# Loading the convolution's weights later and in fewer bytes, and spreading them with smaller copies

## The chip, the cores and the metric

The kernel runs on one core of one Trainium2 chip. The metric is the device time of one execution in microseconds (us); for the kernel before it is 83.28 us, the median of three runs (83.2 to 83.3). The profiled execution took 83.26 us, of which the profile's span covers 82.0 us; times inside the trace are counted from the start of that span.

## The reference

Eight images of 32 channels and 128 x 128 pixels are normalized in 16 groups of two channels each, convolved with a 3 x 3 kernel by way of a 256 x 256 Fourier transform, given a bias and added to the input:

```python
def _gn(v, G=16, eps=1e-5):
    g = v.reshape(B_, G, C_ // G, H_, W_)
    m = jnp.mean(g, axis=(2, 3, 4), keepdims=True)
    s = jnp.var(g, axis=(2, 3, 4), keepdims=True)
    return ((g - m) / jnp.sqrt(s + eps)).reshape(v.shape)

def _L0_conv_ref(x, weight, bias, stride, padding):
    ...                                  # fft_H = fft_W = 256
    fout = jnp.einsum('bihw,oihw->bohw', fx, wf)
    sp = jnp.fft.ifft2(fout, norm='ortho').real
    sh = (fft_H - out_h) // 2            # 64: the crop begins at row and column 64
    out = sp[:, :, sh:sh + out_h, sw:sw + out_w]
    return out + bias[None, :, None, None]

x = x + _L0_conv_ref(_gn(x), L0_conv_weight, L0_conv_bias, 1, 1)
```

Because of the crop, the convolution reaches only a top left quarter (66 x 66) of each output image. Everywhere else the result is the input plus the bias.

## The kernel before

The host splits each image into its four phases (even and odd rows, even and odd columns). A partition is one phase of one channel, so an image is 128 partitions by 64 x 64 numbers. The 3 x 3 convolution becomes four 128 x 128 matrices (`w_sb`, 128 x 512), each used on 33 x 33 positions. Each matrix has the taps of the 3 x 3 kernel at fixed places, repeated for the four output phases, and zeros elsewhere.

On one side the SyncE queue loads the images, on the other the ScalarE queue loads `wb_sb` with the weights and the bias. Its columns are 5 x 3 taps of 32 outputs (the host repeats two rows of taps and puts in a row of zeros, so that each copy below is one regular pattern), the bias and 15 columns of zeros: 32 rows of 496 float32, 62 KB.

```python
loaded[0] = []
for half in range(2):
    rows = slice(half * H // 2, (half + 1) * H // 2)
    loaded[0].append((rows.stop, load(xts[0][:, rows, :], x[0, :, 0, rows, :])))
    if half == 0:
        weights_in = load(wb_sb, wb, by="act")        # the weights: first on ScalarE's queue
for img in range(1, 4):
    loaded[img] = [(H, load(xts[img], x[img // 2, :, img % 2]))]
for pair in range(2, NPAIR):
    loaded[2 * pair] = loaded[2 * pair + 1] = [(H, load(pairs[pair], x[pair]))]
# ... GpSimd builds avg, the matrix that averages over a group's partitions ...
put("act", lambda e: e.activation(warm, eps, AF.Sqrt), eps_ok)   # ScalarE's first activation
```

Then the first image is summed (VectorE: sums; ScalarE: sums of squares), `group` averages over the partitions with a matmul, `take_std` and `normalize` give `g`. In between GpSimd spreads the weights:

```python
pilot(0)                # a matmul on image 0's first pixel
pilot_back(0)           # ScalarE: its result, as an origin for the squares
sum_up(0)               # VectorE, two halves
sum_squares(0)          # ScalarE, two halves
keep_warm(0, 2)         # TensorE: filler matmuls 128 x 512 on avg
group(0, 0)
taps = wb_sb[:, 0 : 15 * C].rearrange("p (a b o) -> p a b o", a=5, b=3)
w5 = w_sb.rearrange("p (dr dc r k) -> p dr dc r k", dr=2, dc=2, r=2)
places = {0: ((0, slice(0, 1), slice(2, 3)), (1, slice(0, 2), slice(0, 2))),
          1: ((0, slice(0, 2), slice(1, 3)), (1, slice(1, 2), slice(0, 1)))}
w_zero = put("pool", lambda e: e.memset(w_sb, 0.0), mark=True)
for q in range(4):                                   # one band of 32 partitions per phase
    rin, cin = q // 2, q % 2
    to = slice(q * C, (q + 1) * C)
    bias_ok = put("pool", ... tensor_copy(bias_sb[to, :], wb_sb[:, 15 * C : 15 * C + 1]), weights_in)
    for dc, c, b in places[cin]:
        w_ok = put("pool", ... tensor_copy(w5[to, :, dc, :, c.start * C : c.stop * C],
                   taps[:, 1 - rin : 5 - rin, b, :]...), w_zero, weights_in)
group(0, 1)
warm_ok = keep_warm(0, 1, w_ok)  # one more filler matmul, only once the weights are spread
pilot(1)                         # needs image 1
take_std(0)                      # ScalarE square, VectorE var, ScalarE std, VectorE rstd, shift
normalize(0)                     # ScalarE, g in two pieces
# ... then, image after image: four products for each of three chunks, addition of ps and bias
# on VectorE, the rest of the image plus bias on GpSimd, the store on SyncE's queue ...
```

The steady part is a loop over the images: TensorE multiplies image i while ScalarE and VectorE sum image i + 2 and normalize image i + 1, and finished images are stored. The last image is stored in parts; the last store waits for the last addition on VectorE.

Of the kernel before, what the change touches and what calls it, by code (L numbers as in the profile page):

```python
# [153 lines left out]
def conv_preact_kernel(nc: bass.Bass, x: bass.AP, wb: bass.AP, out: bass.AP):  # L154
    NPAIR, _, _, H, W = x.shape
    B = 2 * NPAIR
    C = P // 4
# [7 lines left out]
    def sbuf(name, *shape):  # L165
        return nc.alloc_sbuf_tensor(name, list(shape), F32).ap()
# [4 lines left out]
    put = Queues(nc)  # L171
# [1 line left out]
    pairs = [sbuf(f"x{pair}", P, 2, H, W) for pair in range(NPAIR)]  # L173
    xts = [pairs[img // 2][:, img % 2] for img in range(B)]


    wb_sb = sbuf("wb_sb", *wb.shape)
    loaded = {}

    def load(to, of, by="sp"):  # L180
        name = f"load{len(put.sems)}"
        put.semaphore(name)
        return put(by, lambda e: e.dma_start(to, of), adds=name)  # L183

    loaded[0] = []
    for half in range(2):
        rows = slice(half * H // 2, (half + 1) * H // 2)
        loaded[0].append((rows.stop, load(xts[0][:, rows, :], x[0, :, 0, rows, :])))
        if half == 0:
            weights_in = load(wb_sb, wb, by="act")  # L190
    for img in range(1, 4):
        loaded[img] = [(H, load(xts[img], x[img // 2, :, img % 2]))]
    for pair in range(2, NPAIR):
# [12 lines left out]
    half = sbuf("half", P, 2 * C)  # L206
# [3 lines left out]
    bias_sb = sbuf("bias_sb", P, 1)  # L210
# [3 lines left out]
    for step, base in ((-1, 0), (1, 1)):  # L214
# [6 lines left out]
            pair_ok, mark=True,  # L221
# [12 lines left out]
        pair_ok, mark=True,  # L234
    )

    put("act", lambda e: e.activation(warm, eps, AF.Sqrt), eps_ok)  # L237

    gs = [sbuf(f"g{k}", P, N, N) for k in range(2)]

# [70 lines left out]
    def group(img, part=0):  # L311


        last = len(parts(img)) - 1
        of = to_sum(img, part)
        ok = put(
            "pe",
            lambda e: e.matmul(  # L318
                ps_ms[:, 0 : of.shape[1]], avg, of, start=(part == 0), stop=(part == last)
            ),  # L320
            *(sums_ok[img][part :: last + 1]), *([first_ok[img + 1]] if img and img + 1 < B else []),
            avg_ok, *means_read.get(img - 1, ()), mark=part == last,
        )
        if part == last:
            group_ok[img] = ok
# [117 lines left out]
    def keep_warm(first, times, *needs):  # L443
# [14 lines left out]

    taps = wb_sb[:, 0 : 15 * C].rearrange("p (a b o) -> p a b o", a=5, b=3)
    w5 = w_sb.rearrange("p (dr dc r k) -> p dr dc r k", dr=2, dc=2, r=2)
    places = {

        0: ((0, slice(0, 1), slice(2, 3)), (1, slice(0, 2), slice(0, 2))),
        1: ((0, slice(0, 2), slice(1, 3)), (1, slice(1, 2), slice(0, 1))),
    }
    w_zero = put("pool", lambda e: e.memset(w_sb, 0.0), mark=True)
    for q in range(4):
        rin, cin = q // 2, q % 2  # L470
        to = slice(q * C, (q + 1) * C)
        bias_ok = put("pool", lambda e: e.tensor_copy(bias_sb[to, :], wb_sb[:, 15 * C : 15 * C + 1]), weights_in, mark=True)
        for dc, c, b in places[cin]:
            w_ok = put(
                "pool",
                lambda e: e.tensor_copy(  # L476
                    w5[to, :, dc, :, c.start * C : c.stop * C],
                    taps[:, 1 - rin : 5 - rin, b, :].rearrange("p (dr r) b o -> p dr r (b o)", dr=2),
                ),
                w_zero, weights_in, mark=True,  # L480
            )
    group(0, 1)
    warm_ok = keep_warm(0, 1, w_ok)
    pilot(1)
# [41 lines left out]
    xt, to = xts[B - 1], out[NPAIR - 1, :, 1]  # L526
# [67 lines left out]
```

## Time and profile before

| engine | busy us | share of the span |
|---|---|---|
| TensorE, matmuls | 66.8 | 81% |
| VectorE | 50.2 | 61% |
| ScalarE | 47.9 | 58% |
| GpSimd | 31.6 | 39% |
| the 16 DMA engines, SyncE's queue alone | | 96.3% |

Busy time is the time in which an engine worked on an instruction, from its first to its last; a share is over the whole span. The DMA line is the time that the packets of a queue took, as a share of 16 engines times the span. The page also has a picture of the span in 40 slices (about 2.05 us each), where each digit is a busy share in tenths, and the trace can be asked for the same numbers over any stretch of time.

In the lines below, PE is TensorE's matmuls and PEld its weight loads, DVE is VectorE, ACT is ScalarE, POOL is GpSimd, SP is SyncE; a q behind the name is the engine's sequencer, which issues DMAs. L476 is line 476 of the kernel. `w_sb<-wb_sb 32x128` is an instruction that writes `w_sb` from `wb_sb` over 32 partitions and 128 elements in each. In square brackets stands how long the engine was idle before, and what ended it. A wait for several semaphores is put down to the one that came last in the record, which can be the wrong one.

### The profile page before, as it was taken

The page shows a single profiled execution, that of the slowest core. Times are in us where ns is not written, and L with a number is a line of the kernel's source. Part 1 is how long each engine was busy: PE and PEld are TensorE (multiplying, and loading weights), DVE is VectorE, ACT ScalarE, POOL GpSimd, SP SyncE. Part 2 cuts the span into 40 slices and gives each one's busy share as a digit, 9 for nine tenths or more (in the row PEclk, how much of TensorE's full clock was granted, in tenths as well). Part 3 has the DMA queues.
Part 4 walks back from the last instruction along what each step waited for, and adds up shares of the span by engine and source line. Part 5 has one row for each costly group of instructions (what it writes and reads, how often), then busy time and mean ns, then how long its engine had stood idle before and what let it go on. Part 6 is the DMA issues. An engine that isn't in the chain of part 4 may idle for free.

```text
span 82.0 us, 686 instructions
## 1 busy us (share of the span) xinstructions
PE 66.8 (81%) x222; PEld 41.3 (50%) x222; DVE 50.2 (61%) x43; ACT 47.9 (58%) x53; POOL 31.6 (39%) x43
## 2 busy tenths in 40 slices
PE   0009974999999999999999999999999999993000
PEld 0005433566666666666666656666666666660000
DVE  0009936960899499769949995996899324006000
ACT  3307967981699299569947974994798260000000
POOL 6876000004069900106992930490085029400000
PEclk9999998579999999999999999999999999999965
DMA  2899999999979979979959889989979999999995
GB/s 40 299 415 443 463 415 423 447 407 423 551 304 511 479 320 479 511 336 431 511 256 511 383 383 511 447 352 479 463 336 423 423 431 439 431 423 419 397 430 239
DMA packets 2164, 33.62 MB, mean 410 GB/s; under 512 B 296, under 2 KB 330, under 8 KB 500
## 3 DMA queue, kind: packets, MB, share of 16 engines
q1 hardware_dynamic: 2020, 33.36, 96.3%
q0 software_dynamic: 96, 0.19, 0.6%
q10 hardware_dynamic: 48, 0.06, 0.3%
HBM read 16.84 MB, written 16.78 MB: 410 GB/s over the span
## 4 chain that ended last, share of the span: by engine, by line
PE 74%; DMA 14%; DVE 2%; SPq 1%; issue 0%
PE ps L412 73%; DMA x<-x_dram 14%; DVE x L428 2%; PE ps_m L318 1%; SPq L183 1%; PE ps_w L265 0%
## 5 line engine op out<-in xcount | busy, mean ns | idle before, releaser
L412 PE MATMUL ps<-g,w_sb 128*128 128x363 f32 (+1 forms) x192 | 60.7, 473 | 0.1
L412 PEld LDWEIGHTS ps<-g,w_sb 128*128 128x128 f32 x192 | 36.1, 194 | 20.0 <-ACT origin L292 1.4
L283 DVE TENSOR_REDUCE sums<-x 128x1 f32<-128x4096 f32 x7 | 30.9, 4411 | 0.6 <-DMA x<-x_dram 0.6
L394 POOL TENSOR_SCALAR x<-x,bias_sb 128x1984 f32<-128x1984 f32 (+3 forms) x12 | 23.2, 1945 | 18.9 <-ACT origin L292 14.6
L303 ACT ACTIVATE unused<-x,origin 128x4096 f32<-128x4096 f32 (+1 forms) x9 | 30.0, 3330 | 0.3
L428 DVE SCALAR_TENSOR_TENSOR x<-ps,bias_sb,x 128x1089 f32<-128x1089 f32 (+2 forms) x9 | 10.9, 1220 | 7.7 <-PE ps L412 7.7
L373 ACT ACTIVATE g<-x,rstd 128x1089 f32<-128x1089 f32 (+2 forms) x8 | 9.4, 1190 | 3.4 <-DVE rstd L347 3.4
L283 DVE TENSOR_REDUCE first_sums<-x 128x1 f32<-128x2048 f32 x2 | 4.6, 2286 | 6.2 <-DMA x<-x_dram 6.2
L258 POOL COPY sums<-x 128x1 f32<-128x1 f32 x6 | 1.0, 186 | 18.2 <-DMA x<-x_dram 18.2
L335 DVE TENSOR_SCALAR var<-ps_m,square 128x1 f32<-128x1 f32 x8 | 1.8, 219 | 8.2 <-ACT square L330 8.2
L265 PE MATMUL ps_w<-x,avg 128*128 128x1 f32 x4 | 0.9, 304 | 7.1 <-POOL w_sb L476 6.1
L330 ACT ACTIVATE square<-ps_m,origin 128x1 f32<-128x1 f32 x8 | 2.1, 261 | 7.3 <-PE ps_m L318 7.3
L447 PE MATMUL ps<-x,avg 128*128 128x512 f32 x6 | 4.9, 942 | 0.0
L265 PEld LDWEIGHTS ps_w<-x,avg 128*128 128x128 f32 x4 | 0.8, 248 | 7.9 <-POOL w_sb L476 6.1
L318 PEld LDWEIGHTS ps_m<-sums,avg 128*128 128x128 f32 x16 | 2.8, 188 | 2.2 <-DVE x L428 1.0
L341 ACT ACTIVATE std<-var,eps 128x1 f32<-128x1 f32 x8 | 2.4, 294 | 2.3 <-DVE var L335 2.3
L344 DVE RECIPROCAL rstd<-std 128x1 f32<-128x1 f32 x8 | 1.3, 164 | 2.9 <-ACT std L341 2.9
L292 ACT ACTIVATE origin<-ps_w 128x1 f32<-128x1 f32 x2 | 0.3, 160 | 4.0 <-PE ps_w L265 4.0
L476 POOL COPY w_sb<-wb_sb 32x128 f32<-32x128 f32 (+1 forms) x8 | 2.5, 340 | 0.0
L318 PE MATMUL ps_m<-sums,avg 128*128 128x3 f32 x16 | 2.3, 214 | 0.0
L447 PEld LDWEIGHTS ps<-x,avg 128*128 128x128 f32 x6 | 1.5, 287 | 1.0 <-issue 1.0
L237 ACT ACT_TABLE_LOAD x1 | 1.3, 1283 | 1.2 <-PEq L579 1.2
(21 smaller groups left out, 13.3 us busy)
## 6 DMA issues: line engine op xcount, KB each, us to landing
x<-x_dram SPq DMA_DIRECT2D x2, 4096.0 KB, 34.3
out_dram<-x SPq DMA_DIRECT2D x2, 4096.0 KB
x<-x_dram SPq DMA_DIRECT2D x3, 2048.0 KB, 16.0
out_dram<-x SPq DMA_DIRECT2D x3, 2048.0 KB
x<-x_dram SPq DMA_DIRECT2D x2, 1024.0 KB, 6.2
out_dram<-x SPq DMA_DIRECT2D x1, 1056.0 KB
out_dram<-x SPq DMA_DIRECT2D x1, 800.0 KB
out_dram<-x POOLq DMA_DIRECT2D x1, 189.0 KB, 7.7
```

The lines of the kernel that those rows point to most:

```text
L283: lambda e: e.tensor_reduce(to_sum(img, k)[:, 0:1], piece, mybir.AxisListType.X, ALU.add),
L303: lambda e: e.activation(unused[:, rows.start * W : rows.stop * W], piece, AF.Square, bias=origins[img], accum_out=to_sum(img, k)[:, 1:2],),
L318: lambda e: e.matmul(ps_ms[:, 0 : of.shape[1]], avg, of, start=(part == 0), stop=(part == last)),
L330: lambda e: e.activation(squares[img], ps_ms[:, 0:1], AF.Square, bias=origins[img]),
L335: lambda e: e.tensor_scalar(variances[img], ps_ms[:, 1:2], squares[img], None, op0=ALU.subtract),
L341: lambda e: e.activation(stds[img], variances[img], AF.Sqrt, bias=eps, scale=float(FFT * FFT)),
L373: lambda e: e.activation(g[:, rows, :], xt[:, LO + rows.start : LO + rows.stop, LO:W], AF.Identity, bias=rstd[:, 1:2], scale=rstd[:, 0:1],),
L394: put("pool", lambda e: e.tensor_scalar(part, part, 1.0, bias_sb, op0=ALU.mult, op1=ALU.add), *free, mark=mark)
L412: lambda e, k=k, dc=dc, rows=rows, top=top: e.matmul(ps[:, 0:rows, 0 : N - dc], w_sb[:, k * P : (k + 1) * P], g[:, top : top + rows, dc:N] ...
L428: lambda e: e.scalar_tensor_tensor(part, in0=ps, scalar=bias_sb, in1=part, op0=ALU.add, op1=ALU.add),
L447: "pe", lambda e: e.matmul(pss[1][:, 0, :], avg, piece, start=True, stop=True),
L476: lambda e: e.tensor_copy(w5[to, :, dc, :, c.start * C : c.stop * C], taps[:, 1 - rin : 5 - rin, b, :].rearrange("p (dr r) b o -> p dr r ( ...
```

## The change

Three things are changed in the set-up of the weights, and nothing in the loop over the images. The load of `wb_sb` moves behind ScalarE's first activation. What is loaded shrinks to the nine taps and the bias, 32 rows of 289 float32, 37 KB. And since the repeated rows and the zeros are gone, each copy into `w_sb` is split in two by the place of the row: sixteen smaller copies on GpSimd take the place of eight. The four copies of the bias go from GpSimd to VectorE. It is meant to leave the transfer engines to the first image at the start, to move fewer bytes, and to take the bias off GpSimd's list.

```diff
     for half in range(2):
         rows = slice(half * H // 2, (half + 1) * H // 2)
         loaded[0].append((rows.stop, load(xts[0][:, rows, :], x[0, :, 0, rows, :])))
-        if half == 0:
-            weights_in = load(wb_sb, wb, by="act")
...
     put("act", lambda e: e.activation(warm, eps, AF.Sqrt), eps_ok)
 
+    weights_in = load(wb_sb, wb, by="act")
+
...
-    taps = wb_sb[:, 0 : 15 * C].rearrange("p (a b o) -> p a b o", a=5, b=3)
+    taps = wb_sb[:, 0 : 9 * C].rearrange("p (a b o) -> p a b o", a=3, b=3)
...
-        bias_ok = put("pool", lambda e: e.tensor_copy(bias_sb[to, :], wb_sb[:, 15 * C : 15 * C + 1]), weights_in, mark=True)
+        bias_ok = put("dve", lambda e: e.tensor_copy(bias_sb[to, :], wb_sb[:, 9 * C : 9 * C + 1]), weights_in, mark=True)
         for dc, c, b in places[cin]:
-            w_ok = put(
-                "pool",
-                lambda e: e.tensor_copy(
-                    w5[to, :, dc, :, c.start * C : c.stop * C],
-                    taps[:, 1 - rin : 5 - rin, b, :].rearrange("p (dr r) b o -> p dr r (b o)", dr=2),
-                ),
-                w_zero, weights_in, mark=True,
-            )
+            for dr, r, a in places[rin]:
+                w_ok = put(
+                    "pool",
+                    lambda e: e.tensor_copy(
+                        w5[to, dr, dc, r, c.start * C : c.stop * C],
+                        taps[:, a, b, :].rearrange("p a b o -> p a (b o)"),
+                    ),
+                    w_zero, weights_in, mark=True,
+                )
...
         "wb_dram": np.concatenate(
-            [
-                np.insert(weight.transpose(1, 2, 3, 0)[:, [1, 2, 0, 1]], 2, 0, axis=1).reshape(C, 15 * C),
-                np.asarray(L0_conv_bias).reshape(C, 1),
-                np.zeros((C, 15), x.dtype),
-            ],
-            axis=1,
+            [weight.transpose(1, 2, 3, 0).reshape(C, 9 * C), np.asarray(L0_conv_bias).reshape(C, 1)], axis=1
         ),
```

## The prediction

> **What bounds the kernel now.** I read the page's DMA part first, then the same transfers over stretches of time, then the first 14 us engine by engine. The queues, as packets, MB and share of 16 engines' span:
>
> ```profile
> span 82.0 us, 686 instructions
> ...
> q1 hardware_dynamic: 2020, 33.36, 96.3%
> q0 software_dynamic: 96, 0.19, 0.6%
> q10 hardware_dynamic: 48, 0.06, 0.3%
> HBM read 16.84 MB, written 16.78 MB: 410 GB/s over the span
> ```
>
> Queue 1 alone (images in and out) fills 96.3% of the span, all three 97.2%. That leaves 2.8%, or 2.3 us. Where they lie is seen by stretch: the columns are the stretch and its length, the busy time of PE, PEld, DVE, ACT and POOL, TensorE's clock, the DMA share and GB/s.
>
> ```profile
> 0.00:2.00 2.00, 0.00 (x0) 0.00 (x0) 0.00 (x0) 0.75 (x1) 1.25 (x8) 1.00 0.21 33
> 2.00:10.00 8.00, 3.90 (x6) 1.94 (x7) 3.81 (x2) 4.01 (x6) 4.85 (x16) 1.00 0.98 397
> 10.00:20.00 10.00, 8.39 (x26) 5.04 (x24) 5.78 (x5) 6.97 (x9) 0.92 (x2) 0.83 1.02 433
> ...
> 60.00:70.00 10.00, 10.00 (x36) 6.26 (x35) 5.73 (x7) 5.22 (x5) 5.67 (x4) 1.00 0.99 424
> 70.00:76.00 6.00, 4.54 (x17) 2.68 (x15) 1.42 (x2) 0.00 (x0) 0.72 (x2) 1.00 0.99 424
> ```
>
> From 2 us on the share is about 1.0 in every stretch, so the idle 2.3 us lie before the first packets and behind the last. The chain of waits names TensorE (74%) instead, because it follows the instructions back from the last store's issue; but that store, issued at 76.09 us, joins a queue that is still full. The tail shows it:
>
> ```profile
> 76.00:77.00 1.00, 0.00 (x0) 0.00 (x0) 0.06 (x1) 0.00 (x0) 0.00 (x0) 1.00 0.83 342
> 77.00:78.00 1.00, 0.00 (x0) 0.00 (x0) 0.00 (x0) 0.00 (x0) 0.00 (x0) 1.00 1.06 444
> 78.00:79.00 1.00, 0.00 (x0) 0.00 (x0) 0.00 (x0) 0.00 (x0) 0.00 (x0) 0.84 1.04 434
> 79.00:80.00 1.00, 0.00 (x0) 0.00 (x0) 0.00 (x0) 0.00 (x0) 0.00 (x0) 0.50 1.00 422
> ```
>
> After 76.09 us the engines move 0.91 x 342 + 444 + 434 + 422 kB, and another 482 kB after 80 us (the windows of that part give 456, 372 and 135 GB/s over half a us each): 2093 kB. The last store is 1056 KB, 1081 kB. So 1012 kB of older stores lay in front of it, 2.4 us at 420 GB/s. A new transfer needs some of this to get going: the first image load, issued at 0.81 us, moves nothing until 1.5 us and is moving by 2.0 us, so 0.7 to 1.2 us. The compute chain thus has 2.4 - 1.2, about 1 us, of slack at the end. The transfer engines set the time: start-up, then 33.6 MB, then the last landing.
>
> [...] 62 KB on ScalarE's queue landed 3.6 us after issue, while SyncE's half images took 6.2. [...] The granted clock was 0.50 from 14 to 16 us here[...]. [...] the reduction beside the weight copies and the one after them both took 2.29 us.
>
> **The change part by part.**
>
> First, bytes. The load falls from 62 KB to 32 x 289 x 4 = 36,992 bytes from 63,488. At 420 GB/s that is 26.5 kB / 420 = 0.06 us. By the page, queue 10 takes 0.3% of 82 us, 0.25 us (0.20 to 0.29 by its rounding); cut in proportion to the bytes (0.58) it saves 0.10 us. I take -0.08 us on a transfer time that is all on the path.
>
> Second, place. The issue leaves 0.81 us. ScalarE's table load and first activation, which ended at 2.74 us behind the 0.41 us issue, can end about 2.3 us; the issue follows then, or as early as 1 us if the sequencer does not hold it for the running activation. With the measured 3.6 us to landing: 4.6 to 5.9 us, 5.9 taken. In the changed kernel the first half image no longer has the weights in front of it and lands up to 63.5 kB / 420 = 0.15 us earlier; image 1 still has 37 KB in front and gains 0.06. The order of bytes is changed, their sum only by the 0.08 above.
>
> Third, the copies on GpSimd and who waits for them:
>
> ```profile
> 4.46 0.18 POOL L472 COPY bias_sb<-wb_sb 32x1 f32<-32x1 f32 x1 [0.46 <-DMA wb_sb<-wb_dram]
> 4.59 0.62 POOL L476 COPY w_sb<-wb_sb 32x128 f32<-32x128 f32 x2
> 5.27 0.18 POOL L472 COPY bias_sb<-wb_sb 32x1 f32<-32x1 f32 x1
> ...
> 7.00 0.63 POOL L476 COPY w_sb<-wb_sb 32x256 f32<-32x256 f32 x2
> ```
>
> The columns are start, length, instruction. From 4.46 to 7.63 us, 3.17 us in all; 0.81 us from band to band. By shape the means are 180 ns (1 element), 286 (128) and 394 (256): 0.844 ns an element on 180. The new copies are 32, 64, 64 and 128 elements a band: 206 + 233 + 233 + 287 = 959 ns. The old band sums to 860 ns and took 805, so three instructions overlap by 18 ns each; four give 959 - 72 = 887 ns. Four bands: 3.55 us, 0.38 more than before, although the bias copies are gone. With a landing at 5.9 us the last copy ends at 9.5 us instead of 7.63. Who waits is TensorE:
>
> ```profile
> 11.03 0.38 PE L318 MATMUL ps_m<-first_sums,avg 128*128 128x2 f32 x2 [0.53 <-ACT unused L303]
> 11.28 1.10 PE L447 MATMUL ps<-x,avg 128*128 128x512 f32 x2
> 13.39 0.38 PE L265 MATMUL ps_w<-x,avg 128*128 128x1 f32 x2 [1.00 <-DMA x<-x_dram]
> 13.84 0.94 PE L412 MATMUL ps<-g,w_sb 128*128 128x363 f32 x1
> ```
>
> The filler at 11.28 us is the first to need the weights, and it starts there because of the statistics in front of it. The convolution starts at 13.84 us because image 1 lands at 13.36. So 9.5 us is 1.8 us early. Even a filler moved to 12.29 us would end by 13.39.
>
> Fourth, the bias on VectorE. The copies stand behind both reductions, which end at 10.76 us, and in front of `var` at 11.75. The trace has a VectorE copy of one element at 145 ns; four make 0.58 us, to 11.34. `var` waits for ScalarE's square, which ends at 11.71, so 0.37 us remain; 0.3 if the chain comes earlier with image 0.
>
> Sum: bytes -0.08 us; place, GpSimd and VectorE 0.00, all beside other work. 83.28 - 0.08 = 83.2 us.
>
> **The rivals.** (A) The weights come late and a wait for them takes the place of the wait for image 1. For it: whole images with larger rows are queued by then, and the little transfer that GpSimd issues at 19.03 us lands only after 6.6 us. With 6.6 in place of 3.6 us the landing is 2.3 + 6.6 = 8.9, the copies end at 12.45, the filler at 13.55, so the convolution starts 0.16 us late[...]. Against it: that transfer is on the queue that the page calls software_dynamic, not on a hardware one. And about 1 us of slack at the end takes it up: 83.2 still. It would need a landing after 10 us to show, and then VectorE's in-order wait for the bias would hold `var` too; say 84.
>
> (B) The start-up gets shorter. From 1.5 to 3.0 us the windows show only 131, 139 and 158 GB/s, 214 kB where 420 GB/s would be 630, so 1.0 us is lost there, and the weight load is in it. If its small rows hold up the first image packets, moving it gives 0.1 to 0.4 us: 82.8 to 83.1. Against it: first packets have their own latency, and the 37 KB then land in full traffic, where nothing hides them. If the old ones were hidden in the ramp, the change costs up to 37 / 420 = 0.09 us instead: 83.4.
>
> (C) TensorE is the bound after all, as its 74% of the chain suggests. Then the time follows image 1's landing, 0.06 us earlier: 83.2 as well. A clock that changes around 14 us could move the compute chain by 1 us in either direction; only a delay above the slack would be seen.
>
> **Range and chances.** The centre is 83.2 us. (B) gives both ends, with repeated runs spread over 0.1 us: 82.9 to 83.5 us, 8 times in 10. The limits of 2% are 81.6 and 84.9 us. Nothing I find gives 1.6 us: faster 1%. Slower needs (A) with a landing after 10 us[...]: 2%. Within 2%: 97%.
>
> **What would show it.** In the changed profile: queue 10 at 0.04 MB and 0.1 to 0.2%; the DMA share still about 1.0 from 2 us to 80 us; GpSimd's sixteen copies over 3.4 to 3.7 us, ending by 10 us; the filler at about 11.2 us with the statistics, not the weights, in front of it; the bias copies between 10.6 and 11.4 us; `var` following the square at once; the convolution starting within 0.2 us of 13.8. It is wrong if the filler starts behind the last copy and the convolution with it, if `var` stands behind a bias copy, if the windows from 1.5 to 3 us move well over 214 kB, or if the DMA share has a hole before 80 us.

## The result and the profile after

The changed kernel takes 83.84 us (median of six runs, 83.8 to 84.24), the kernel before 83.22 (six runs of the same comparison): a ratio of 1.0081, 95% interval 1.0062 to 1.0100. It is 0.6 us slower, small but well outside the noise, and outside the predicted range of 82.9 to 83.5.

The page of the changed kernel, its span and its queues (packets, MB, share of 16 engines' span):

```profile
span 82.1 us, 695 instructions
...
q1 hardware_dynamic: 2020, 33.36, 96.3%
q0 software_dynamic: 96, 0.19, 0.6%
q10 hardware_dynamic: 48, 0.04, 0.1%
HBM read 16.81 MB, written 16.78 MB: 409 GB/s over the span
```

The first line is the riddle: the span is 82.1 us against 82.0, so the profiled program hardly changed while the measured time went up by 0.6. The queues are as foreseen. So are the stretches (length, busy PE, PEld, DVE, ACT, POOL, clock, DMA share, GB/s), full to the end:

```profile
10.00:20.00 10.00, 9.46 (x28) 5.72 (x27) 6.28 (x10) 7.14 (x11) 0.92 (x2) 1.00 1.02 436
...
60.00:70.00 10.00, 10.00 (x36) 6.25 (x35) 4.94 (x7) 4.43 (x5) 5.60 (x5) 1.00 0.99 423
70.00:76.00 6.00, 3.75 (x15) 2.16 (x13) 1.48 (x2) 0.00 (x0) 0.00 (x0) 1.00 0.99 423
```

And so is the set-up, in the timeline of the changed kernel (start, length, instruction, idle time in front):

```profile
0.95 0.38 ACTq L182 DMA_DIRECT2D wb_sb<-wb_dram  x1
...
5.19 3.33 POOL L476 COPY w_sb<-wb_sb 32x32 f32<-32x32 f32 x16 [1.19 <-DMA wb_sb<-wb_dram]
5.78 2.29 DVE L282 TENSOR_REDUCE first_sums<-x 128x1 f32<-128x2048 f32 x1 [5.78 <-DMA x<-x_dram]
...
10.47 0.66 DVE L471 COPY bias_sb<-wb_sb 32x1 f32<-32x1 f32 x4
...
11.26 2.06 PE L446 MATMUL ps<-x,avg 128*128 128x512 f32 x2
11.44 0.26 ACT L329 ACTIVATE square<-ps_m,origin 128x1 f32<-128x1 f32 x1 [0.68 <-PE ps_m L317]
11.74 0.22 DVE L334 TENSOR_SCALAR var<-ps_m,square 128x1 f32<-128x1 f32 x1 [0.60 <-ACT square L329]
...
13.63 5.54 PE L411 MATMUL ps<-g,w_sb 128*128 128x363 f32 x14
```

The copies end at 8.52 us, long before the filler at 11.26. The bias copies end at 11.13; `var` follows the square. The convolution starts at 13.63 us, 0.2 earlier than before. GpSimd waits longer for the weights (1.19 us against 0.46), but nothing on the way to the end does.

So the loss has to lie outside the span. The profiled executions took 83.26 us (before) and 83.80 (after); less 82.0 and 82.1 that leaves 1.3 and 1.7 us beside the span. The trace can be asked for stretches behind its last instruction. The changed kernel:

```profile
83.00:83.50 0.50, 0.00 (x0) 0.00 (x0) 0.00 (x0) 0.00 (x0) 0.00 (x0) 0.50 0.00 0
83.50:84.00 0.50, 0.00 (x0) 0.00 (x0) 0.00 (x0) 0.00 (x0) 0.00 (x0) 0.50 0.05 16
```

16 GB/s over half a us is 8 KB, about 1.7 us behind the last instruction of a kernel that has nothing left to move. The list of queues for 82 to 86 us says what it is:

```profile
DMA packets 1, 0.01 MB, mean 2 GB/s; under 512 B 0, under 2 KB 0, under 8 KB 0
## 3 DMA queue, kind: packets, MB, share of 16 engines
q14 instruction: 1, 0.01, 0.6%
```

A queue 14 of kind "instruction", one packet. (Both kernels have six such packets of 8 KB before the span starts.) The same question to the kernel before:

```profile
DMA packets 0, 0.00 MB, mean 0 GB/s; under 512 B 0, under 2 KB 0, under 8 KB 0
```

Theory T, a guess from that packet: an engine's instructions come in blocks of the packet's size; the change made one engine's stream longer, past the end of a block, and behind the span something then waits for the next block to be fetched. The trace records 686 instructions before and 695 after, waits and DMA issues included: four more on VectorE (45 to 49, the bias copies) and five more on GpSimd (58 to 63: eight copies more, four bias copies fewer, one wait more). Rivals: P, the later load itself costs; V, the bias copies on VectorE cost; N, each further instruction costs something outside the span. Of T the two traces show the packet and the counts. The block, the engine and the wait they do not show, nor a reason to expect 0.6 us.

### The profile page after: what moved, and what is told of

The parts are those of the page before. It is cut to its first block, busy times and chain, and to the rows that moved or that the text cites. A ratio compares the mean times of both kernels' runs of the same rounds, so it can differ in the third digit from the quotient of the medians.

```text
span 82.1 us, 695 instructions
## 1 busy us (share of the span) xinstructions
PE 67.3 (82%) x222; PEld 41.5 (51%) x222; DVE 50.7 (62%) x47; ACT 47.9 (58%) x53; POOL 31.8 (39%) x47
## 4 chain that ended last, share of the span: by engine, by line
PE 77%; DMA 9%; DVE 5%; SPq 0%; issue 0%
PE ps L411 72%; DMA x<-x_dram 9%; DVE first_sums L282 3%; PE ps L446 2%; PE ps_m L317 2%; DVE x L427 2%; PE ps_w L264 1%; SPq L182 0%; DVE bias_sb L471 0%
## 5 line engine op out<-in xcount | busy, mean ns | idle before, releaser
L446 PE MATMUL ps<-x,avg 128*128 128x512 f32 x6 | 5.8, 1108 | 0.0
L476 POOL COPY w_sb<-wb_sb 32x64 f32<-32x64 f32 (+2 forms) x16 | 3.2, 236 | 1.4 <-DMA wb_sb<-wb_dram 1.2
L317 PEld LDWEIGHTS ps_m<-first_sums,avg 128*128 128x128 f32 x4 | 1.2, 324 | 1.7 <-ACT unused L302 1.1
```

Source lines behind the costliest of these rows:

```text
L317: lambda e: e.matmul(ps_ms[:, 0 : of.shape[1]], avg, of, start=(part == 0), stop=(part == last)),
L446: "pe", lambda e: e.matmul(pss[1][:, 0, :], avg, piece, start=True, stop=True),
L476: lambda e: e.tensor_copy(w5[to, dr, dc, r, c.start * C : c.stop * C], taps[:, a, b, :].rearrange("p a b o -> p a (b o)"),),
```

## The experiments

All ratios are to the kernel before on the same chip, with 95% intervals, as recorded; they differ from the quotient of the two medians by up to 0.003. Each run's short diff is against the kernel before or, where said, the changed one.

**One part of the change alone, and length alone.** The load moved, the rest as before (e1_place):

```diff
-        if half == 0:
-            weights_in = load(wb_sb, wb, by="act")
...
     put("act", lambda e: e.activation(warm, eps, AF.Sqrt), eps_ok)
+    weights_in = load(wb_sb, wb, by="act")
```

> The kernel before with one part of the change: the 62 KB load moved behind ScalarE's first activation. Theory T (the lost 0.6 us lie behind the span, where an instruction fetch on queue 14 appeared because GpSimd's program grew from 58 to 63 instructions): the count is unchanged, so no fetch behind the span and 83.2 us. Rival P (the later load is the cause): 83.8 us.

Measured 83.26 us, ratio 0.9993 (0.9982 to 1.0004); no packet between 82 and 86 us. Rival P falls.

The bias copies on VectorE, the rest as before (e2_bias):

```diff
-        bias_ok = put("pool", ...
+        bias_ok = put("dve", ...
```

> The kernel before with one part of the change: the four copies of the bias on VectorE, so that VectorE's program grows by 4 instructions and GpSimd's shrinks by 4. Theory T with GpSimd as the engine: 83.2 us, no fetch behind the span. Theory T with VectorE as the engine, or rival V (bias copies on VectorE delay something): 83.8 us, and under T a fetch behind the span.

Measured 83.36 us, ratio 1.0003 (0.9991 to 1.0015); no packet. Rival V falls, and with it VectorE as T's engine.

The kernel before with five idle instructions more (e3_pool5):

```diff
         adds="moved",
     )
+    spare = sbuf("spare", P, 5)
+    for k in range(5):
+        put("pool", lambda e: e.memset(spare[:, k : k + 1], 0.0))
     sum_squares(1)
```

> The kernel before with nothing of the change, but five one-element memsets of a spare tile on GpSimd while it waits for image 2 (at about 19 us). Theory T with GpSimd as the engine: 83.8 us, the span within 0.1 us of 82.0, and one fetch of 8 KB on queue 14 about 1.7 us behind the span. Rivals P and V: 83.2 us, no fetch.

Measured 83.97 us, ratio 1.0079 (1.0061 to 1.0098): the whole loss, without any of the change. The five memsets take 0.25 us at 19.7 us, in a pause of GpSimd that lasts until 23.1. The span is 82.0 us, and behind it the queue list of this run shows

```profile
DMA packets 2, 0.02 MB, mean 4 GB/s; under 512 B 0, under 2 KB 0, under 8 KB 0
## 3 DMA queue, kind: packets, MB, share of 16 engines
q14 instruction: 2, 0.02, 1.5%
```

Two packets here against one in the changed kernel.

The changed kernel with its last five weight copies left out, which brings GpSimd back to 58 instructions and leaves parts of the matrices zero (e4_eleven; diff against the changed kernel):

```diff
             for dr, r, a in places[rin]:
+                copies += 1
+                if copies > 11:
+                    continue
                 w_ok = put(
```

> The changed kernel with eleven of its sixteen weight copies (the last five are left out, so a part of the matrices stays zero and the convolution is incomplete). GpSimd's program is back at 58 instructions; load, bytes and bias copies are those of the change. Theory T with GpSimd as the engine: 83.2 us and no fetch behind the span. Rivals P and V: 83.8 us.

Measured 83.25 us, ratio 0.9998 (0.9986 to 1.0011); no packet behind the span. The load's place, its 37 KB and the bias copies are all in it, and the loss is gone.

**Step or slope, and which engines.** The whole change, complete, with half of the weight copies moved to VectorE, 55 instructions on GpSimd (e5_split; diff against the changed kernel):

```diff
-                    "pool",
+                    "pool" if q < 2 else "dve",
...
-    warm_ok = keep_warm(0, 1, w_ok)
+    warm_ok = keep_warm(0, 1, half_ok, w_ok)      # half_ok: the last copy on GpSimd
...
```

> The whole change, complete, but with eight of the sixteen weight copies (the two bands of odd rows) on VectorE behind its two reductions, so that GpSimd's program has 55 instructions. Theory T with GpSimd's instruction stream as the cause: 83.2 us and no fetch behind the span; the copies hold up var by 0.5 to 1 us, which the slack at the end takes up. If the 0.6 us belonged to the change's work in any other way, 83.8 us. This run also says what the change is worth without the fetch: by the record -0.08 us, so a ratio of 0.999.

Measured 83.48 us beside 83.39 for the kernel before, ratio 1.0001 (0.9971 to 1.0030); no packet. The copies do delay the chain, by less than expected, as the timeline of this run shows:

```profile
11.54 0.50 DVE L476 COPY w_sb<-wb_sb 32x128 f32<-32x128 f32 x4
12.07 0.22 DVE L334 TENSOR_SCALAR var<-ps_m,square 128x1 f32<-128x1 f32 x1
```

`var` comes 0.32 us later than before (12.07 against 11.75), and nothing of it reaches the end. The interval is too wide to tell -0.08 us from nothing.

Three spare memsets instead of five (e6_pool3, the diff of e3_pool5 with 3):

> The kernel before with three spare memsets on GpSimd instead of five (61 instructions). If the cost is a step at a block of the instruction stream, the time is either 83.2 or 83.85 us and nothing between, the latter with a fetch on queue 14 behind the span. If every instruction costs something outside the span, 3/5 of 0.65: 83.6 us.

Measured 83.98 us, ratio 1.0064 (1.0047 to 1.0081), one packet on queue 14 behind the span. As much as with five: a step.

Six spare activations on ScalarE, and eighteen spare memsets on VectorE, each bringing its engine to 63 instructions (e7_act6, e8_dve18):

```diff
     put("act", lambda e: e.activation(warm, eps, AF.Sqrt), eps_ok)
+    spare = sbuf("spare", P, 6)                   # 18
+    for k in range(6):                            # 18
+        put("act", lambda e: e.activation(spare[:, k : k + 1], eps, AF.Sqrt))
+                                                  # "dve", e.memset(spare[:, k : k + 1], 0.0)
```

> The kernel before with six spare one-element activations on ScalarE behind its first one, where it is idle (57 + 6 = 63 instructions in its program, as many as GpSimd's in the changed kernel). If all engines have the same limit: 83.85 us and a fetch behind the span. If only GpSimd's stream stands close to a limit here: 83.2 us and no fetch.

> The kernel before with eighteen spare one-element memsets on VectorE before image 0 lands (45 + 18 = 63 instructions in its program). As with ScalarE: 83.85 us and a fetch behind the span if all engines have the same limit, 83.2 us if only GpSimd's stream stands close to one.

ScalarE: 83.39 us, ratio 0.9999 (0.9980 to 1.0019). VectorE: 83.65 us, ratio 1.0029 (1.0013 to 1.0045). Neither has an instruction packet behind the span, but each has one inside it, between 71 and 72 us and between 54 and 55 us. I had expected either the full step or nothing; the run on VectorE is between, and its loss is inside a span of 82.4 us. The limit of 58 is thus GpSimd's own in this kernel. Whether ScalarE or VectorE has such a step at another count stays open: VectorE went through 49 (e2_bias) and 57 (e5_split) without loss, and ScalarE was run with 57 and 63 only. Whose packets those two are, the traces don't say.

**How far beyond the limit.** One spare memset on GpSimd (e9_pool1), twenty (e10_pool20) and sixty (e11_pool60), by the diff of e3_pool5:

> The kernel before with one spare memset on GpSimd (59 instructions in its program). Theory T says only that the step lies between 58 and 61: either 83.2 us without a fetch behind the span or 83.85 us with one. A value between the two would speak for a cost per instruction.

> The kernel before with twenty spare memsets on GpSimd (78 instructions). If the cost comes from where the end of an 8 KB block falls, and the instructions that close the program behind the kernel's own are fewer than about 18, the end of the block now falls inside the span, the fetch moves there and is hidden: 83.2 to 83.5 us, a fetch on queue 14 before 82 us. If they are more, the time is 83.85 us with the fetch still behind the span. Rival N (any longer program costs more): at least 83.85 us, rather more than with five.

> The same with sixty spare memsets (118 instructions), which end near 23 us, before GpSimd's large additions are due. Block theory: the end of the block falls well inside the span, no fetch behind the span, 83.2 to 83.5 us, so more instructions cost less than five do. Rival N: more than 83.85 us.

One: 83.89 us, ratio 1.0060 (1.0039 to 1.0080). A single instruction in a pause (0.12 us, the mean of the sixty memsets in e11_pool60) cost 0.5 us. Its one profile was odd, with no packet of queue 14 behind the span and a span of 82.5 us. Twenty: 83.35 us, ratio 1.0000 (0.9979 to 1.0022). Twenty more instructions cost nothing where one cost half a us. The queue list of that run for 56 to 57 us shows where the packet went:

```profile
q1 hardware_dynamic: 15, 0.49, 114.6%
q14 instruction: 1, 0.01, 1.9%
```

It lies in the middle of the images' traffic, and none lies behind the span. Rival N falls. Sixty: 83.97 us, ratio 1.0048 (1.0024 to 1.0072), runs scattered from 83.37 to 84.36. The packet moved further forward, to between 23 and 24 us, as T with its blocks would have it, and the 1.2 us beside the span (84.2 less 83.0) are those of the kernel before. But the span of the profiled run was 83.0 us, and the twenty executions have spans from 82.1 to 83.1, so this kernel loses time inside, for a reason these runs don't show. My 83.2 to 83.5 us missed it.

**The same limit in the changed kernel.** The change with twenty spare memsets (e12_after20), and the change with twelve of its copies, 59 instructions, four copies left out (e13_twelve: the diff of e4_eleven with 12); then the kernel before with two spare memsets (e14_pool2), for the odd profile of the run with one:

> The whole change with twenty spare memsets added on GpSimd while it waits for image 2 (83 instructions in its program). Block theory: as with twenty on the kernel before, the end of the block falls inside the span, no fetch lies behind it, 83.2 to 83.5 us: the change loses its cost by getting longer. Rival N, or a cause in the change's own work: at least 83.84 us.

> The changed kernel with twelve of its sixteen weight copies (four are left out; the convolution is incomplete), one more than in the run with eleven: 59 instructions in GpSimd's program. If the limit lies between 58 and 59, whatever the instructions are: 83.85 us, against 83.25 us with eleven. If it was crossed by chance in the run with one spare memset: 83.25 us.

> The kernel before with two spare memsets on GpSimd (60 instructions). The run with one took 83.89 us, but its profile showed no fetch behind the span, only 0.24 us more behind the span than the kernel before, and a span of 82.5 us. If that was a chance of one execution, this one shows the fetch behind the span, a span within 0.15 us of 82.05 and 83.9 us. If a limit crossed by so little acts inside the span, again a span near 82.5 us without a fetch behind it.

The change made longer: 83.35 us, ratio 0.9994 (0.9967 to 1.0020). The packet lies between 40 and 41 us, and none behind the span:

```profile
q14 instruction: 1, 0.01, 1.9%
```

Twelve copies: 83.86 us, ratio 1.0065 (1.0049 to 1.0081), where eleven took 83.25. Its queue list behind the span:

```profile
DMA packets 1, 0.01 MB, mean 2 GB/s; under 512 B 0, under 2 KB 0, under 8 KB 0
## 3 DMA queue, kind: packets, MB, share of 16 engines
q14 instruction: 1, 0.01, 0.7%
```

Two memsets: 84.00 us, ratio 1.0068 (1.0044 to 1.0092), a packet behind the span and a span of 82.2 us, so the missing packet in the run with one wasn't a rule.

All profiled executions side by side, in the order of GpSimd's instructions; the last column is the time less the span, whose rounding leaves 0.1 us of doubt:

| kernel | GpSimd's instructions | profiled us | span us | 8 KB instruction packet | beside the span, us |
|---|---|---|---|---|---|
| e2_bias | 55 | 83.36 | 82.1 | none | 1.3 |
| e5_split | 55 | 83.30 | 82.0 | none | 1.3 |
| before | 58 | 83.26 | 82.0 | none | 1.3 |
| e1_place | 58 | 83.29 | 82.1 | none | 1.2 |
| e4_eleven | 58 | 83.24 | 82.0 | none | 1.2 |
| e7_act6 | 58 | 83.47 | 82.2 | inside | 1.2 |
| e8_dve18 | 58 | 83.68 | 82.4 | inside | 1.2 |
| e9_pool1 | 59 | 84.00 | 82.5 | none recorded | 1.5 |
| e13_twelve | 59 | 83.91 | 82.1 | behind | 1.8 |
| e14_pool2 | 60 | 84.00 | 82.2 | behind | 1.8 |
| e6_pool3 | 61 | 84.00 | 82.1 | behind | 1.9 |
| e3_pool5 | 63 | 83.90 | 82.0 | behind, two | 1.9 |
| after | 63 | 83.80 | 82.1 | behind | 1.7 |
| e10_pool20 | 78 | 83.37 | 82.1 | inside | 1.3 |
| e12_after20 | 83 | 83.22 | 82.0 | inside | 1.2 |
| e11_pool60 | 118 | 84.20 | 83.0 | inside | 1.2 |

With an instruction packet behind the span, 1.7 to 1.9 us lie beside it; with none, or one inside, 1.2 to 1.3. That holds for the kernel before and the changed one alike, with one exception in a single profile (e9_pool1). The span is on record for 380 executions in all. In the 61 with 59 to 63 instructions on GpSimd, 1.48 to 2.02 us lie beside it; in the 319 others, with 55 to 58 or with 78 and more, 1.18 to 1.31. The odd profile of e9_pool1 is the lowest of its eleven, and the other ten have 1.68 to 1.91. No version beat the kernel before by more than its interval.

The traces also hold semaphore events behind the last recorded instruction: fourteen of one semaphore in each profile, in nearly the same rhythm. With 55 to 58 instructions or with 78 and more, the last comes 1.43 to 1.46 us behind the span. With 63 instructions (the changed kernel and e3_pool5) the row stands still between the seventh and the eighth, for 0.23 and 0.24 us in place of 0.04; with 61, between the eleventh and the twelfth, for 0.30 in place of 0.04. With 59 and 60 the row is as before, and shows nothing of the loss, which presumably lies behind its last event. So the longer GpSimd's program, the earlier in the closing part comes the halt, as it would if the end of a block were reached there. But the packet starts only 1.67 to 1.70 us behind the span, when those halts are over (1.34 to 1.35, and 1.61): it goes with the crossing, and these halts are no wait for its landing.

## Why the prediction was wrong

The bound was right. The transfer engines are full from 2 to 80 us in both kernels (a share of 1.00 in each, 424 and 423 GB/s). The strongest sign came unasked: in the changed kernel the last addition ended at 75.27 us instead of 76.06, and the span did not get shorter. (Part of it goes with TensorE's clock. The view prints 1.00 for it from 10 to 20 us, but this trace's clock record begins at 15.84 us. The 128x363 matmuls that started before 15.5 us took 0.8 to 0.9 us, as in the 0.50 stretch of the kernel before, and those from 16.0 us on 0.46 to 0.47. In the kernel before, that slow stretch ended only at 17.24 us.) The slack at the end is real in the other direction too: with six activations on ScalarE (e7_act6) the last store was issued at 77.51 us instead of 76.09, and the span was 82.2 us, 0.2 more.

The place: the issue left at 0.95 us, the early one of the two cases named, beside the table load rather than behind the activation. The landing was at 5.14 us, within 4.6 to 5.9 us; it came 4.2 us after the issue, where 3.6 had been an estimate from the load at its old place. The copies: 3.33 us against 3.55 predicted, ending 1 us earlier than the 9.5 named. The bias: 0.66 us against 0.58, starting 0.13 us before the stretch named, and `var` did not wait for it. The filler started at 11.26 us, with the statistics in front of it. Rivals (A) and (C) did not happen. Of (B), the windows from 1.5 to 3.0 us moved 270 kB (147, 82 and 311 GB/s) instead of 214, one of the signs named for being wrong, and the half images landed 6.0 us after issue in the median instead of 6.2. At the end that is not to be seen: the span stayed at 82.1 us.

The bytes, -0.08 us: queue 10 fell from 0.3% to 0.1% as named. In the time it is not resolved: the two complete versions of the change without the packet behind the span stand at 1.0001 (0.9971 to 1.0030) and 0.9994 (0.9967 to 1.0020), which hold 0.999 and 1.000 alike.

The step that failed is the third, as it stood in the sum: "bytes -0.08 us; place, GpSimd and VectorE 0.00, all beside other work. 83.28 - 0.08 = 83.2 us." It weighed GpSimd's sixteen copies by their time alone, which is hidden, and carried the 1.3 us beside the span over unchanged. The runs put another term in its place: five more instructions in GpSimd's program, one of which was already too many, and with them 0.5 to 0.7 us more beside the span, with an 8 KB packet on the queue of kind "instruction" behind it. None of the rivals had it, since all of them looked for a wait inside the span. The view that could have warned was at hand: the difference of 83.26 and 82.0 us showed that 1.3 us of the metric lie where the page shows nothing.

That the crossing of GpSimd's limit, from 58 to 59 instructions, causes the loss is shown, by adding (1.0060 with one memset) and by taking away (1.0065 with twelve copies, 0.9998 with eleven), in both kernels. What is waited for behind the span is open. That a block of GpSimd's instructions ends there is inferred from the packet and from the halts, which come earlier as the program gets longer; no instruction behind the span is recorded, and the packet starts too late to be what the recorded halts wait for.

## What to carry to other kernels

Compare the time with the span before looking for a wait: if the time changed and the span did not, look at what lies behind the last instruction, and at queues other than the kernel's own. The number of instructions on GpSimd cost time here though every one of them was hidden, in a step and not in proportion, and past the step it was free again: the ratio was 1.0060 with one more, 1.0079 with five more and 1.0000 with twenty more. A small change that turns few instructions into many is worth counting per engine, and is worth testing against the kernel before with as many idle instructions added.

## What was not expected of the hardware

- An 8 KB instruction packet behind the span goes with about 0.5 us more beside it (1.7 to 1.9 against 1.2 to 1.3 us in the profiles); inside the span it can go unnoticed (0.9994 and 1.0000 in time). With sixty memsets on GpSimd (packet at 23 to 24 us) and eighteen on VectorE (54 to 55 us) the spans were 83.0 and 82.4 us; whether the packet has to do with that is open.
- The DMA issue on ScalarE's queue did not wait for the engine's work in front of it: it left at 0.95 us, while the table load ran from 0.81 to 2.09 and the activation from 2.10. So it was in all six profiles with the load at its new place.
- Moving the load alone did not bring the first half images in earlier (6.2 us after issue in the median, as before). With 37 KB, five profiles give 5.9 to 6.0 us; with 62 KB at the old place, ten give 6.0 to 6.3, so the gain is hardly more than the scatter.
